# Layer 1's weighted sums in four column groups of TensorE, and the keys' loads on ScalarE's queue

## The chip, the cores and the metric

The kernel runs on one core of a Trainium2 chip. The metric is device time in microseconds (us), from one execution; the median of several is compared. Engines in the text: TensorE (PE in the profile; its weight loads are PEld), VectorE (DVE), ScalarE (ACT), GpSimd (POOL), SyncE (SP). A name with a q (SPq, ACTq) is that engine's sequencer, which issues DMAs.

## The reference

Two graph layers in fp32 over 16 graphs of 1024 nodes with 256 features. `adj` is an int32 matrix of 1024 x 1024 for each graph, zeros and ones here. Cut to what matters:

```python
h = relu(layernorm(x))
# layer 0: 8 heads of 32 features
Q, K, V = h @ Wq.T + bq, h @ Wk.T + bk, h @ Wv.T + bv       # split into heads
scores = where(adj == 0, -inf, Q @ K.T * 32 ** -0.5)          # per head, 1024 x 1024
x = x + concat(softmax(scores) @ V) @ Wo.T + bo
# layer 1: one head; adj chooses one of four edge vectors a_0 to a_3
h = relu(layernorm(x))
e_k = leaky_relu((h * a_k) @ h.T, 0.2)
scores = where(adj == 1, e_0, ..., where(adj == 4, e_3, -9e15))
x = x + softmax(scores) @ h
```

Layer 1's last line is what the change is about: for 128 queries at a time, probabilities (128 queries x 1024 nodes) times node features (1024 x 256), then a division by each query's sum and the residual.

## The kernel before

The work is cut into 128 blocks of 128 queries (16 graphs x 8 blocks). The main loop runs over steps `s`, one block each, and inside a step over the 8 heads `h`. A step carries several blocks at different stages at once, as a pipeline written out by hand (the order in the source is the order on every engine):

- `now` and `was` (class `Attend`): layer 0 of block `s`, and the end of block `s - 1`. For each head: scores on TensorE (L400, an fp32r matmul), the running maximum on VectorE (L412), the exponential on ScalarE (L420), then a turn of the probabilities so that nodes lie on partitions. Heads 1, 3, 5, 7 are turned by TensorE transposes (L512) and ScalarE copies (L513), heads 0, 2, 4, 6 by VectorE in 32 x 32 blocks (L345) and four DMAs that place the blocks (`placed`, L350). `combine` (L455) then sums the values, four heads at a time in four column groups of TensorE, each writing 32 partitions of `sums_place`; `combined` (L465) divides, `output` (L470) is the last matmul of layer 0, `residual` (L476) adds x and starts the norm, whose small steps run on GpSimd (L145 to L161); `normed` (L491) and `turn_normed` (L498, L502) make layer 1's features.
- `edge` and `edge_was` (class `Edges`): layer 1 of a block nine steps behind. `score` (L541), maximum and exponential, `turn_blocks` and `place_blocks` (VectorE and four DMAs into `pT1`, one buffer), then, one step later, `gather` (L581). Here the features are TensorE's weights and the turned probabilities stream, so the sums come out with features on partitions: `gathered` (L588) copies them to SBUF on ScalarE, `turn_back` (L593) turns them with two transposes into `brief`, and `store` (L597 to L600) divides, adds x and writes out, one step later still (`edge_last`).
- `piece`, `piece_was` (class `Piece`): keys, queries and values of a block nine steps ahead. `turn` (L224) transposes its features into `brief`, `turned` (L236, L237) copies them to SBUF twice on ScalarE, `project` (L254) makes keys and queries, `high` (L270, ScalarE) and `split` (L275, VectorE) cut them into two parts that go to DRAM (`write_keys` L299, `qd` L292).

Four places of 128 x 256 fp32 in PSUM are shared by hand. They are the halves of two banks: `sums_place` and `brief` in one, `early` and `late` in the other. Semaphores are put in by the framework, so that accesses to one bank by different engines follow the order of the source:

```python
banks = [ps_acc.tile([P, 2, D], F32, tag=f"acc{i}", ...) for i in range(2)]
sums_place, brief, early, late = (banks[i // 2][:, i % 2, :] for i in range(4))
```

The keys of a graph are 8 tiles of 128 x 1024 (one for each head), each in one buffer. `load_key` (L329) fetches them from DRAM: those of heads 0 to 5 of the next graph in the last step of a graph, two heads after their last use, those of heads 6 and 7 in the first step of the new graph. These DMAs, and nearly all others, are issued by SyncE; ScalarE issues the second copy of the keys' halves (`write_keys(1)`). After the loop a few small instructions test whether the graph has edges of kinds other than 1, for which a general path exists that these inputs do not take.

Of the kernel before, what the change touches and what calls it, by code (L numbers as in the profile page):

```python
# [42 lines left out]
def gnn_kernel(  # L43
# [42 lines left out]
    sums_place, brief, early, late = (banks[i // 2][:, i % 2, :] for i in range(4))  # L86
    sums_place = by_chunk(sums_place)

# [83 lines left out]
    class Piece:  # L172
# [42 lines left out]
        def turn(self):  # L215
            self.hT = self.buffer(2, [P, NC, self.n * P])
            self.hTm = self.buffer(4, [P, NC, self.n * P])
            for c in range(NC):
                if self.n > 1:
                    tr = ps_tr.tile([P, self.n, P], F32, tag="tr", name="trn0")  # L220
                elif c == 0:
                    tr = by_chunk(brief)
                for t in range(self.n):
                    nc.tensor.transpose(  # L224
                        tr[:, c if self.n == 1 else t, :], self.h[:, t, c * P : (c + 1) * P], ident
                    )
                if self.n > 1:
                    nc.scalar.copy(self.hT[:, c, :], tr.rearrange("p t n -> p (t n)"))
                    nc.vector.tensor_copy(
                        self.hTm[:, c, :].rearrange("p (t k b) -> p t k b", t=self.n, b=NB),  # L230
                        tr.rearrange("p t (b k) -> p t k b", b=NB),
                    )
            self.h_ps = tr
# [92 lines left out]
    def load_key(b, h):  # L326
        kt = keys.tile([P, N], F32R, tag=f"k{h}", name=f"k{h}_{b}")
        c, r = divmod(h, GROUP)
        nc.sync.dma_start(  # L329
            out=kt.bitcast(F32),  # L330
# [28 lines left out]
    class Attend:  # L359
# [87 lines left out]
        def turned_reciprocals(self):  # L447
            self.recT = work.tile([P, NC, P], F32, tag="cT", name="recT", bufs=1)
            nc.scalar.copy(self.recT, self.rec_ps)

        def combine(self, g):
            for j in range(NT):
                for r in range(GROUP):
                    h = g * GROUP + r
                    nc.tensor.matmul(  # L455
                        sums_place[r * HD : (r + 1) * HD, g, :],
                        lhsT=vs[self.b][:, j, place_of(h) : place_of(h) + HD],
# [5 lines left out]
        def combined(self):  # L463
            self.oT = work.tile([P, NC, P], F32, tag="oT")
            nc.vector.tensor_tensor(self.oT, sums_place, self.recT, ALU.mult)  # L465

# [49 lines left out]
    class Edges:  # L516
# [60 lines left out]

        def gather(self, c):

            for j in range(NT):  # L580
                nc.tensor.matmul(  # L581
                    sums_place[:, c, :], lhsT=h1s[self.b][:, j, c * P : (c + 1) * P], rhs=self.pT[:, j],
                    start=(j == 0), stop=(j == NT - 1),
                )

        def gathered(self):
            self.o1T = work.tile([P, NC, P], F32, tag="cT", name="o1T", bufs=1)
            nc.scalar.copy(self.o1T, sums_place)  # L588

        def turn_back(self):  # L590
            self.o = brief
            for c in range(NC):
                nc.tensor.transpose(self.o[:, c * P : (c + 1) * P], self.o1T[:, c, :], ident)  # L593

        def store(self):
            rec = small.tile([P, 1], F32, tag="rec1")
            nc.vector.reciprocal(rec, self.total)  # L597
            ot = work.tile([P, D], F32, tag="ot")
            nc.vector.scalar_tensor_tensor(ot, self.o, rec, self.x1, ALU.mult, ALU.add)  # L599
            nc.sync.dma_start(out=out[self.b, self.rows, :], in_=ot)  # L600
# [79 lines left out]
    with tc.manual_schedule():  # L680
# [21 lines left out]
        for piece in first:  # L702
            piece.values()
        piece, edge, edge_was, edge_last = piece_next, None, None, None
        now.load_queries()
# [10 lines left out]
        for s in range(B * NT + LAG + 1):  # L716
            b, t = divmod(s, NT)
            nxt, edge_nxt, piece_nxt = attend_of(s + 1), edges_of(s + 1), piece_of(s + 1)
            for h in range(HEADS):
# [4 lines left out]
                if now:  # L724
                    now.scores(h)
                    if h >= 2 and t == NT - 1 and b + 1 < B:
                        load_key(b + 1, h - 2)
                    if h < 2 and t == 0 and b > 0:
                        load_key(b, HEADS - 2 + h)
                if h == 0 and piece_was:  # L730
                    piece_was.split()
                if h == 1 and edge_last:
                    edge_last.store()
                if h == 1 and piece_was:
# [11 lines left out]
                if h == 6 and piece_was:  # L746
                    piece_was.split()
                    piece_was.split()
                if now:
                    now.softmax_max(h)  # L750


                if h == 7 and edge_was:
                    edge_was.gathered()
                if ending:
# [3 lines left out]
                if h == 7 and was:  # L759
                    was.normed()  # L760


                if h == 5 and piece:
                    piece.turn()
                if turning and th in BY_BLOCKS:
# [41 lines left out]
                if h == 4:  # L807
# [9 lines left out]
                    if edge_nxt:  # L817
                        edge_nxt.prepare()
                if h == 5:
                    if edge_was:  # L820
                        edge_was.gather(0)
# [15 lines left out]
                if h == 7:  # L837
                    if now:
                        now.combine(0)
                    if edge_nxt:  # L840
                        edge_nxt.mask()
                    if edge_was:
                        edge_was.turn_back()
                    if edge:
# [7 lines left out]
            gone, was, now = was, now, nxt  # L852
            edge_last, edge_was, edge = edge_was, edge, edge_nxt
            piece_was, piece = piece, piece_nxt

        edge_last.store()

# [51 lines left out]
```

## Time and profile before

| | us |
|---|---|
| median of 3 runs | 3425.91 (3419.38 to 3431.87) |
| profiled execution, its own time | 3418.87 |
| its span, first to last instruction | 3417.0 |
| busy: TensorE, VectorE, ScalarE, GpSimd | 3107.9, 2777.9, 2449.8, 2176.1 |
| DMA | 829.70 MB, mean 243 GB/s |
| mean granted TensorE clock | 0.979 |

A line of the page's groups reads: line, engine, operation, out<-in by the program's names, partitions x elements and type, how many; then after the bar the busy time of all in us and the mean of one in ns; after the next bar the idle time of the engine just before them, with what ended most of it. A row of the timeline is: start in us from the span's beginning, length in us, engine, line, operation, how many merged into the row, and in brackets the idle time ahead of it. fp32 matmuls appear as two records each, one for each pass over the data.

### The profile page before, as it was taken

To read this page: it belongs to the slowest core of one execution; us is meant where nothing else is said; L and a number is where in the kernel's file an instruction comes from. 1 tells how busy PE (TensorE), PEld (TensorE's weight loads), DVE (VectorE), ACT (ScalarE), POOL (GpSimd) and SP (SyncE) were. 2 spreads that over 40 slices of the span, in tenths; PEclk is the share of its full clock that TensorE was granted. 3 is DMA by queue.
4 is the path that set the end of the run, shared out by engine and by line. 5 is a ranking of instruction groups with operands and counts; after the bars stand their busy time and mean duration, and the time that the engine had idled before them with its cause. 6 is when DMAs were issued, how large, how long until landed. Compare 5 with 4: busy or idle time off the path is not lost. (4 is left out here: it accounts for less than half of the span.)

```text
span 3417.0 us, 92640 instructions
## 1 busy us (share of the span) xinstructions
PE 3107.9 (91%) x32178; PEld 2474.1 (72%) x32178; DVE 2777.9 (81%) x5111; ACT 2449.8 (72%) x4957; POOL 2176.1 (64%) x5274
## 2 busy tenths in 40 slices
PE   5778989899999999999899898999999999898987
PEld 3666777777777777777777777777777777776765
DVE  3778878788787888888888787888878788788873
ACT  3777777677676777767777676777767777777761
POOL 2456767667666766767667666766766666665553
PEclk8999999999999999999999999999999999999999
DMA  6778888888888888888888888888888888888764
GB/s 222 210 234 237 237 265 245 267 237 250 262 238 263 248 262 247 241 268 246 266 238 249 264 235 265 247 262 245 242 264 241 273 237 241 270 235 263 205 180 112
DMA packets 855754, 829.70 MB, mean 243 GB/s; under 512 B 73840, under 2 KB 804080, under 8 KB 855280
## 3 DMA queue, kind: packets, MB, share of 16 engines
q1 hardware_dynamic: 786800, 788.02, 77.1%
q10 hardware_dynamic: 68480, 35.67, 3.5%
q8 instruction: 260, 4.26, 0.5%
q14 instruction: 214, 1.75, 0.2%
HBM read 320.08 MB, written 167.77 MB: 143 GB/s over the span
## 5 line engine op out<-in xcount | busy, mean ns | idle before, releaser
L420 ACT ACTIVATE p<-p,nmx 128x1024 f32<-128x1024 f32 x1024 | 1181.2, 1154 | 361.1 <-DVE nmx L412 356.6
L412 DVE CUSTOM_DVE_ANT_0 p<-s,neg 128x1024 f32<-128x1024 f32 x1024 | 1242.7, 1214 | 193.6 <-PE s L400 172.3
L400 PE MATMUL s<-k,qt 128*128 128x512 f32 x2048 | 775.4, 460 | 24.9 <-DVE nmx L412 17.8
L455 PE MATMUL acc<-pT,v 128*32 128x128 f32 x16384 | 560.9, 281 | 91.7 <-DMA pT<-blocks 89.6
L345 DVE STREAM_TRANSPOSE blocks<-p 128x1024 f32<-128x1024 f32 x512 | 634.9, 1240 | 0.0
L382 POOL TENSOR_SCALAR neg<-adj 128x1024 bf16<-128x1024 int32 x128 | 467.9, 3655 | 213.9 <-DMA adj<-in_adj 210.9
L581 PE MATMUL acc<-pT,h 128*128 128x128 f32 x4096 | 512.1, 279 | 80.4 <-ACT hTm L237 68.4
L455 PEld LDWEIGHTS acc<-pT,v 128*32 128x32 f32 x16384 | 469.2, 113 | 155.7 <-issue 144.7
L581 PEld LDWEIGHTS acc<-pT,h 128*128 128x128 f32 x4096 | 480.0, 193 | 135.0 <-ACT hTm L237 115.9
L513 ACT COPY pT<-trp 128x512 f32<-128x512 f32 x1024 | 540.4, 578 | 33.4 <-DMA kd<-halves 18.2
L512 PE MATMUL trp<-ident,p 128*128 128x128 f32 x4096 | 537.7, 275 | 18.5 <-ACT p L420 17.7
L512 PEld LDWEIGHTS trp<-ident,p 128*128 128x128 f32 x4096 | 472.6, 141 | 90.8 <-ACT p L420 47.1
L535 POOL TENSOR_SCALAR neg<-adj 128x1024 bf16<-128x1024 int32 x128 | 469.2, 3666 | 39.9 <-DMA adj<-in_adj 30.4
L541 PE MATMUL s<-h1T,ha 128*128 128x512 f32 x1024 | 480.3, 592 | 0.5 <-ACT h1T L502 0.5
L400 PEld LDWEIGHTS s<-k,qt 128*128 128x128 f32 x2048 | 329.2, 192 | 141.1 <-DVE nmx L412 74.2
L439 POOL COPY wide<-rec 128x256 f32<-128x256 f32 x128 | 50.8, 397 | 520.5 <-DVE rec L437 487.6
L155 POOL TENSOR_TENSOR sq<-r 128x1 f32<-128x1 f32 (+1 forms) x750 | 247.5, 330 | 60.5
L541 PEld LDWEIGHTS s<-h1T,ha 128*128 128x128 f32 x1024 | 184.0, 190 | 136.9 <-issue 123.7
L554 DVE CUSTOM_DVE_ANT_0 sel<-s,neg 128x1024 f32<-128x1024 f32 x128 | 156.8, 1225 | 63.8 <-PE s L541 53.8
L420 ACT ACTIVATION_READ_ACCUMULATOR p<-p,nmx 128x1 f32 x1024 | 201.2, 197 | 0.0
L157 POOL TENSOR_SCALAR sq<-sq 128x1 f32<-128x1 f32 (+1 forms) x750 | 158.4, 211 | 65.7
L158 POOL TENSOR_TENSOR r<-r,sq 128x1 f32<-128x1 f32 (+1 forms) x750 | 151.0, 201 | 62.5
(104 smaller groups left out, 3952.6 us busy)
## 6 DMA issues: line engine op xcount, KB each, us to landing
pT<-blocks SPq DMA_DIRECT2D x2560, 128.0 KB, 3.2
adj<-in_adj SPq DMA_DIRECT2D x256, 512.0 KB, 5.2
qt<-qd SPq DMA_DIRECT2D x128, 512.0 KB, 6.3
k<-kd SPq DMA_DIRECT2D x128, 512.0 KB, 5.9
qd<-halves SPq DMA_DIRECT2D x240, 256.0 KB, 2.9
kd<-halves ACTq DMA_DIRECT2D x240, 128.0 KB, 3.0
kd<-halves SPq DMA_DIRECT2D x240, 128.0 KB, 2.6
xb<-in_x SPq DMA_DIRECT2D x128, 128.0 KB, 2.6
```

Of the source, the lines that this page charges most:

```text
L155: g.tensor_tensor(sq, r, r, ALU.mult)
L345: nc.vector.transpose(blocks.rearrange("p b j q -> p j b q"), p)
L382: nc.gpsimd.tensor_scalar(self.neg, self.adj, 0.0, MASKED, ALU.is_equal, ALU.mult)
L400: nc.tensor.matmul(self.ps[:, cols], lhsT=self.qt[:, h, :], rhs=keysets[self.b][h][:, cols], start=True, stop=True,)
L412: nc.vector.tensor_tensor_reduce(out=p, in0=sides[h in (3, 5, 7)], in1=self.neg, scale=-SCALE, scalar=FLOOR, op0=ALU.add, op1=ALU.min, acc ...
L420: nc.scalar.activation(p, p, AF.Exp, bias=nmx, scale=-1.0, accum_out=self.sums[:, h : h + 1])
L455: nc.tensor.matmul(sums_place[r * HD : (r + 1) * HD, g, :], lhsT=vs[self.b][:, j, place_of(h) : place_of(h) + HD], rhs=self.turned[h][:, j ...
L512: nc.tensor.transpose(tr[:, j, :], p[:, jj * P : (jj + 1) * P], ident)
L513: copy(pT[:, half * 4 : half * 4 + 4, :], tr)
L535: nc.gpsimd.tensor_scalar(self.neg, self.adj, 0.0, MASKED, ALU.is_equal, ALU.mult)
L541: nc.tensor.matmul(self.e[:, cols], lhsT=self.ha[:, c, :], rhs=h1Ts[self.b][:, c, cols], start=(c == 0), stop=(c == NC - 1),)
L581: nc.tensor.matmul(sums_place[:, c, :], lhsT=h1s[self.b][:, j, c * P : (c + 1) * P], rhs=self.pT[:, j], start=(j == 0), stop=(j == NT - 1),)
```

## The change

Layer 1's `gather` now takes the turned probabilities as weights, 32 queries for each of TensorE's four column groups, and streams the features, 256 columns at a time. The sums come out with queries on partitions, straight in `sums_place`. The two calls no longer take one half of the features each, but one half of the nodes each. `gathered` and `turn_back` go, and `store` reads `sums_place` in the same step (head 7, ahead of VectorE's maximum) where it read `brief` in the next one (head 1). `Piece.turn` for the pieces of the main loop writes to `late` where it wrote to `brief`, and comes behind the head's transposes at head 5 where it came ahead of them. `load_key` issues from ScalarE's queue, behind the head's exponential, and each key comes one head later: heads 0 to 4 in the last step of a graph, heads 5 to 7 in the first step of the next. The reciprocals' tile `recT` has a buffer of its own.

```diff
     sums_place, brief, early, late = (banks[i // 2][:, i % 2, :] for i in range(4))
-    sums_place = by_chunk(sums_place)
...
                 elif c == 0:
-                    tr = by_chunk(brief)
+                    tr = by_chunk(late)
                 for t in range(self.n):
...
         c, r = divmod(h, GROUP)
-        nc.sync.dma_start(
+        nc.scalar.dma_start(
             out=kt.bitcast(F32),
...
         def turned_reciprocals(self):
-            self.recT = work.tile([P, NC, P], F32, tag="cT", name="recT", bufs=1)
+            self.recT = work.tile([P, NC, P], F32, tag="recT", bufs=1)
             nc.scalar.copy(self.recT, self.rec_ps)
...
                     nc.tensor.matmul(
-                        sums_place[r * HD : (r + 1) * HD, g, :],
+                        sums_place[r * HD : (r + 1) * HD, g * P : (g + 1) * P],
                         lhsT=vs[self.b][:, j, place_of(h) : place_of(h) + HD],
...
             self.oT = work.tile([P, NC, P], F32, tag="oT")
-            nc.vector.tensor_tensor(self.oT, sums_place, self.recT, ALU.mult)
+            nc.vector.tensor_tensor(self.oT, by_chunk(sums_place), self.recT, ALU.mult)
...
-        def gather(self, c):
-
-            for j in range(NT):
-                nc.tensor.matmul(
-                    sums_place[:, c, :], lhsT=h1s[self.b][:, j, c * P : (c + 1) * P], rhs=self.pT[:, j],
-                    start=(j == 0), stop=(j == NT - 1),
-                )
-
-        def gathered(self):
-            self.o1T = work.tile([P, NC, P], F32, tag="cT", name="o1T", bufs=1)
-            nc.scalar.copy(self.o1T, sums_place)
-
-        def turn_back(self):
-            self.o = brief
-            for c in range(NC):
-                nc.tensor.transpose(self.o[:, c * P : (c + 1) * P], self.o1T[:, c, :], ident)
+        def gather(self, half):
+
+            for j in range(half * NT // 2, (half + 1) * NT // 2):
+                for a in range(NB):
+                    nc.tensor.matmul(
+                        sums_place[a * HD : (a + 1) * HD, :], lhsT=self.pT[:, j, a], rhs=h1s[self.b][:, j, :],
+                        start=(j == 0), stop=(j == NT - 1),
+                    )
...
             ot = work.tile([P, D], F32, tag="ot")
-            nc.vector.scalar_tensor_tensor(ot, self.o, rec, self.x1, ALU.mult, ALU.add)
+            nc.vector.scalar_tensor_tensor(ot, sums_place, rec, self.x1, ALU.mult, ALU.add)
             nc.sync.dma_start(out=out[self.b, self.rows, :], in_=ot)
...
             piece.values()
-        piece, edge, edge_was, edge_last = piece_next, None, None, None
+        piece, edge, edge_was = piece_next, None, None
         now.load_queries()
...
                     now.scores(h)
-                    if h >= 2 and t == NT - 1 and b + 1 < B:
-                        load_key(b + 1, h - 2)
-                    if h < 2 and t == 0 and b > 0:
-                        load_key(b, HEADS - 2 + h)
                 if h == 0 and piece_was:
                     piece_was.split()
-                if h == 1 and edge_last:
-                    edge_last.store()
                 if h == 1 and piece_was:
...
                     piece_was.split()
+                if h == 7 and edge_was:
+                    edge_was.store()
                 if now:
...
-                if h == 7 and edge_was:
-                    edge_was.gathered()
                 if ending:
...
-
-                if h == 5 and piece:
-                    piece.turn()
+                if now and h >= 3 and t == NT - 1 and b + 1 < B:
+                    load_key(b + 1, h - 3)
+                if now and h < 3 and t == 0 and b > 0:
+                    load_key(b, HEADS - 3 + h)
+
+
                 if turning and th in BY_BLOCKS:
...
                 if h == 5:
+                    if piece:
+                        piece.turn()
                     if edge_was:
...
                         edge_nxt.mask()
-                    if edge_was:
-                        edge_was.turn_back()
                     if edge:
...
             gone, was, now = was, now, nxt
-            edge_last, edge_was, edge = edge_was, edge, edge_nxt
+            edge_was, edge = edge, edge_nxt
             piece_was, piece = piece, piece_nxt
-
-        edge_last.store()
...
         seen = small.tile([P, B], F32, tag="seen", bufs=1)
```

## The prediction

> **What bounds the kernel now.** I read the page first, then the waits, then TensorE's timeline over two ordinary steps, then a step at which the graph changes. The page and the list of waits (who waited for whom: us in total, times, longest):
>
> ```profile
> PE 3107.9 (91%) x32178; PEld 2474.1 (72%) x32178; DVE 2777.9 (81%) x5111; ACT 2449.8 (72%) x4957; POOL 2176.1 (64%) x5274
> L455 PE MATMUL acc<-pT,v 128*32 128x128 f32 x16384 | 560.9, 281 | 91.7 <-DMA pT<-blocks 89.6
> L581 PE MATMUL acc<-pT,h 128*128 128x128 f32 x4096 | 512.1, 279 | 80.4 <-ACT hTm L237 68.4
> k<-kd SPq DMA_DIRECT2D x128, 512.0 KB, 5.9
> ACT o1T L588 <- PE acc L581: 148.8, 127, 11.4
> PE acc L581 <- ACT hTm L237: 68.4, 109, 0.7
> PE acc L455 <- DMA pT<-blocks: 89.6, 51, 5.2
> ```
>
> TensorE is nearly always busy. Matmuls are pipelined, so I price them from start to start in the timeline (start, us, then what runs, and in brackets the idle time before it):
>
> ```profile
> 1610.63 1.88 PE L541 MATMUL s<-h1T,ha 128*128 128x512 f32 x4
> ...
> 1619.37 1.13 PE L470 MATMUL acc<-woT,oT 128*128 128x256 f32 x4 [0.32 <-DVE oT L465]
> 1620.14 0.82 PE L400 MATMUL s<-k,qt 128*128 128x512 f32 x2
> 1620.86 0.44 PE L224 MATMUL acc<-ident,h 128*128 128x128 f32 x2
> 1621.14 1.04 PE L512 MATMUL trp<-ident,p 128*128 128x128 f32 x8
> 1622.01 1.95 PE L581 MATMUL acc<-pT,h 128*128 128x128 f32 x16
> 1623.72 0.71 PE L400 MATMUL s<-k,qt 128*128 128x512 f32 x2
> 1625.12 2.05 PE L581 MATMUL acc<-pT,h 128*128 128x128 f32 x16 [0.69 <-ACT hTm L237]
> 1627.02 1.06 PE L254 MATMUL acc<-hT,wkT 128*128 128x128 f32 x8
> ...
> 1629.34 1.96 PE L455 MATMUL acc<-pT,v 128*32 128x128 f32 x64
> 1631.22 0.44 PE L593 MATMUL acc<-ident,o1T 128*128 128x128 f32 x2
> 1631.41 0.71 PE L400 MATMUL s<-k,qt 128*128 128x512 f32 x2
> ...
> 1635.23 1.88 PE L541 MATMUL s<-h1T,ha 128*128 128x512 f32 x4
> ```
>
> A step is 24.60 us (1610.63 to 1635.23), and in it TensorE idles about 1.0: 0.32 for VectorE, 0.69 ahead of the second gather. The first step of a new graph is longer. The same row starts at 1477.09 and again, a step later, at 1508.48: 31.39 us. In between stands this:
>
> ```profile
> 1486.06 0.41 PE L455 MATMUL acc<-pT,v 128*32 128x128 f32 x4
> 1490.27 3.63 PE L455 MATMUL acc<-pT,v 128*32 128x128 f32 x60 [3.80 <-DMA pT<-blocks]
> ```
>
> Over the 15 such steps the starts of the first maximum (L412) give 98 us more than 15 times 24.6. VectorE had turned head 6 by 1479.79; SyncE issued its four placing DMAs only at 1485.39 to 1487.87, behind key loads and waits for landings. So two things bound the kernel: TensorE in ordinary steps, SyncE's queue and the DMAs at the change of graph.
>
> **What the Trainium skill says.** The Trainium skill, "PSUM — Partial Sum Buffer", section "PSUM bank collisions raise a hardware error": two engines must be kept apart by bank and quadrant, not by address. The trace agrees: `sums_place` and `brief` are halves of one bank, and the second gather waits 0.69 us for a ScalarE copy out of `brief` that it needs no data from. The Trainium skill, "TensorEngine Tiling (Array Packing)", Key Properties: changing the tiling mode drains the array. Around L455 the trace agrees: its quads of four column groups start 109 ns apart, but about 0.09 us is lost on the way in and 0.11 on the way out. The Trainium skill, "DMA: Bandwidth & Descriptors", Issuing engines are not separate DMA queues: another issuing engine saves its sequencer's time alone, since all use the same 16 DMA engines. The trace has no key on ScalarE's queue. The Trainium skill, "TensorE: Matmul & The Clock Gate", Part 1: after some 3.4 us of idleness the clock halves. It does here: 0.59 and 0.56 granted in the two stretches of 4 us from 1488, and the 60 matmuls above took 3.63 instead of about 1.9 us.
>
> **The change, part by part.** All in the ordinary step first.
>
> - The gather. Before, 16 matmul records of 128 columns took 1.71 us (1622.01 to 1623.72), 107 ns each. After, a half has 4 blocks by 4 groups by 2 passes, 32 records of 256 columns, in 8 quads. L455 shows that four groups of fp32 run together at the price of one (109 against 107), so a quad of 256 columns costs 2 x 107 + 2 = 216 ns, and a half 1.73, with 0.2 for entry and exit 1.93. That is +0.22 for each, against the undisturbed 1.71. Bounds: 1.71 if the switch hides, 2.15 if it costs twice as much or quads space out; never near four times, as L455 excludes serial groups.
> - `turn_back` (L593) goes: 1631.22 to 1631.41, -0.19. ScalarE's copy L588 goes (0.37) with its stall (148.8 / 127 = 1.17 each). ScalarE then waits there for GpSimd's `shift` (124.6 us in the list already), so I count nothing for it.
> - The false wait goes: the second gather shares no bank with `late`. Its -0.69 and the restart (1.90 instead of 1.71, -0.19) are gained. hT must now be ready for L254 only, and its copies end at 1625.07, before the new gather does.
> - `piece.turn` (L224) goes behind the transposes, into `late`, which VectorE's residual (L476, 1621.53 to 1621.92) must have read. TensorE gets there at 1621.73: a new wait of 0.2 to 0.3, with the gather and head 6's scores queued behind it. ScalarE's `high` comes at 1623.91, later than all this.
> - The store (0.12 + 0.48 us of VectorE) moves from head 1 to head 7. There VectorE idles 1.09 ahead of L412 for scores, so it is covered; it ends near 1628.0, before the next L455 needs its bank (1629.07). At head 1 it only lengthens VectorE's wait for L541 (0.31). Its DMA is the same one, earlier in SyncE's order.
>
> In order from 1610.63: L470 stays at +8.74 (VectorE sets it), L512 at +10.23, L224 at +11.4, gather +11.7 to +13.6, scores to +14.2, gather to +16.1, L254 +16.9, L400 +17.4, L512 +18.4, L455 +20.3, then 3.8 to the next L541: 24.1. Gain 0.5 per step, 0 to 0.8 with the bounds. GpSimd's own loop (VectorE's reciprocals, 16.7 us of GpSimd, 2 of ScalarE, VectorE's head 0 and 1) is some 24.1 us now and loses the store's 0.6: it doesn't become the bound. Over some 110 steps: **-55** (0 to -88).
>
> The keys. SyncE loses 8 issues of about 0.65 us at each change of graph, 5.2 in all, about what it was late. If head 6's DMAs go 3 to 4 us earlier, up to the 3.8 wait and the 1.7 of slow clock come back, 5.5. But both queues' DMAs carry eight semaphores in turn, and each waits for the landing of the DMA eight before it in program order. ScalarE's sequencer then holds all that is behind it:
>
> ```profile
> 1637.74 0.52 ACTq L299 DMA_DIRECT2D kd<-halves  x1
> 1638.46 1.07 ACT L513 COPY pT<-trp 128x512 f32<-128x512 f32 x2 [1.72 <-DMA pT<-blocks]
> ```
>
> Counting the new order, key 1 waits for `qt` (1.6 us of ScalarE, of which VectorE's idle 1.1 for `halves` hides most), and key 4 for key 3 itself: 5.9 to land, less 2.8 between two exponentials, 3.1, of which 1.5 is hidden by VectorE's idle time at head 0. Cost some 2.1, up to 5.7 if nothing hides. The issues themselves (0.5 each) lie beside a running exponential of 1.15. Net 5.5 - 2.1 = 3.4 at best; since the DMA engines are 0.97 busy there and the bytes stay, I take 2: 15 x 2 = **-30** (+60 to -75).
>
> The end loses L588, L593 and their hand-overs, -1.
>
> Sum: -55 - 30 - 1 = -86, against the profiled execution's 3418.87 us: 3333. That execution lies 7 us below the median of the runs shown (3425.91), so I say 3340.
>
> **Rivals.**
> - Only TensorE's part counts; the DMA engines set the change of graph as before. For it: 0.97 busy from 1458 to 1500. 3425.9 - 56 = 3370.
> - Only the keys count; TensorE's switches cost the full bound and a VectorE or GpSimd chain takes the rest. For it: VectorE has no idle time from 1612.66 to 1623.71. 3425.9 - 31 = 3395, and if the keys help little too, no change.
> - Slower: key loads hold ScalarE. Each change of graph pays 5.7 and SyncE's relief doesn't reach TensorE, since the blocks placed still wait for eight-deep landings. 15 x 5.7 = 86, less 35 of a smaller TensorE gain: +51, 3477. It decides from about 3.7 us per change of graph (55 / 15). For it: the 1.72 above, and 3.37 us of ScalarE idle at 1480.05 behind such an issue. Against it: GpSimd holds ScalarE at head 7 anyway.
>
> **How the numbers follow.** The forecast gets 0.42, the first rival 0.15, the second 0.15 (0.1 of it no change), the slower one 0.28. A measurement of this kernel can tell about 0.3%, 10 us, from no change. Faster 0.42 + 0.15 + 0.05 = 0.62, same 0.10, slower 0.28. The forecast's own range is 3290 to 3385; to leave out no more than 2 in 10 it must reach into the slower case: 3275 to 3445.
>
> **What would show it.** Right: the gather's row with 8192 records of 128*32 and 128x256, a half taking 1.85 to 2.0 us from start to start, no wait of it for L237; a step of about 24.1; the first step of a graph under 30; L455's waits for pT under 50 us in total. Wrong: halves above 2.15; a step still of 24.6; a new wait of ScalarE behind `k<-kd` issues above 60 us in total, with VectorE waiting for ScalarE's `halves` or exponentials in the last step of a graph.

## The result and the profile after: slower

The changed kernel takes 3547.57 us (median, 3546.29 to 3553.22), the kernel before, run beside it, 3427.92 (3419.38 to 3431.87): a ratio of 1.0356, with a 95% interval of 1.0332 to 1.0379. The forecast was 3340, and the result lies above its whole range. The span went from 3417.0 to 3546.5 us.

Lines of the changed kernel are mostly one lower than before (L412 is now L411, L513 is L512, L237 is L236). First the lines of its page that answer to those shown of before:

```profile
PE 3166.9 (89%) x36018; PEld 2259.1 (64%) x36018; DVE 2783.2 (78%) x5111; ACT 2418.5 (68%) x4829; POOL 2177.0 (61%) x5274
L454 PE MATMUL acc<-pT,v 128*32 128x128 f32 x16384 | 558.0, 284 | 18.6 <-DMA pT<-blocks 9.8
L581 PE MATMUL acc<-h,pT 128*32 128x256 f32 x8192 | 518.3, 388 | 11.1 <-DMA pT<-blocks 9.9
k<-kd ACTq DMA_DIRECT2D x128, 512.0 KB, 6.1
```

The edits did what they say. The gather has 8192 records of 128x256 in column groups and no wait for ScalarE's copy of hT; the keys go out on ScalarE's queue; and TensorE's waits of L455 for placed blocks fell from 89.6 to 9.8 us. Yet the run is longer. The list of waits of the changed kernel (who waited for whom: us in total, times, longest) shows what came in their place:

```profile
POOL neg L381 <- DMA adj<-in_adj: 274.8, 120, 14.7
ACT h L490 <- POOL shift L160: 185.0, 100, 13.0
PE trp L511 <- ACT p L419: 174.0, 107, 5.5
DVE halves L274 <- ACT hTm L236: 163.1, 119, 6.9
ACT pT L512 <- DMA pT<-blocks: 110.2, 40, 4.9
ACT pT L512 <- DMA kd<-halves: 81.1, 63, 2.8
```

(`hTm` is one of ScalarE's two copies of layer 0's turned features, `halves` are the parts of keys and queries, `kd<-halves` is a key write, `trp` and `pT` are turned probabilities before and after ScalarE's copy.) In the kernel before, these waits read:

```profile
POOL neg L382 <- DMA adj<-in_adj: 210.9, 93, 11.1
ACT h L491 <- POOL shift L161: 124.6, 120, 3.0
PE trp L512 <- ACT p L420: 17.7, 33, 1.4
ACT pT L513 <- DMA pT<-blocks: 6.8, 7, 1.7
ACT pT L513 <- DMA kd<-halves: 18.2, 38, 1.1
```

VectorE had no wait for hTm. TensorE's wait for it (68.4) is gone, and VectorE has one of 163.1, while its wait for ScalarE's `halves` fell from 149.7 to 61.2. TensorE's wait for exponentials is ten times what it was.

I measure a step from the start of one block's first maximum (L412, L411) to the next block's, and take apart three kinds (means, in us). The table adds up to the span's 129.5:

| | before | after | times | sum |
|---|---|---|---|---|
| ordinary step | 24.53 | 24.97 | 90 | +40 |
| last step of a graph | 25.71 | 28.44 | 14 | +38 |
| first step of a graph | 31.34 | 33.49 | 14 | +30 |
| the start: from the span's beginning to the first maximum | 70.6 | 79.8 | 1 | +9 |
| first nine steps together | 206.1 | 209.5 | 1 | +3 |
| the tail: from the last layer-0 step's start to the end | 133.8 | 142.6 | 1 | +9 |

The last and first steps of a graph are where the eight keys are loaded. ScalarE's timeline there (start, us, what runs, idle time before it in brackets):

```profile
1525.38 0.33 ACTq L328 DMA_DIRECT2D k<-kd  x1
1525.81 0.60 ACT L209 ACTIVATE h<-xin,shift,r 128x256 f32<-128x256 f32 x1 [4.63 <-DMA pT<-blocks]
...
1541.20 0.52 ACTq L298 DMA_DIRECT2D kd<-halves  x1
1541.88 0.51 ACTq L328 DMA_DIRECT2D k<-kd  x1
1542.42 0.37 ACT L501 COPY h1T<-acc 128x256 f32<-128x256 f32 x1 [4.67 <-PE s L540]
...
1548.21 0.52 ACTq L298 DMA_DIRECT2D kd<-halves  x1
1548.77 0.67 ACTq L328 DMA_DIRECT2D k<-kd  x1
1549.61 0.59 ACT L512 COPY pT<-trp 128x512 f32<-128x512 f32 x1 [4.54 <-DMA pT<-blocks]
```

Key 1 could be issued only at 1525.38, when `qt`, issued by SyncE at 1517.16 and eight DMAs ahead in program order, had landed (1525.36). ScalarE stood still for 4.63 us (the label names a placed block; what stands ahead of L209 in ScalarE's order is the key); over the 14 last steps it stands still there for 3.9 us on average. In the first step of the new graph it is mainly the second key write that holds ScalarE, twice. The one at 1541.20 waits for a block's DMA that lands at 1541.12, the one at 1548.21 for the write eight DMAs ahead, issued by SyncE at 1542.96, which lands only at 1548.13, among the keys. The key that is issued right behind each write adds 0.7 and 0.9 us. TensorE's timeline shows who paid:

```profile
1551.87 1.97 PE L511 MATMUL trp<-ident,p 128*128 128x128 f32 x8 [5.19 <-ACT p L419]
```

In such first steps TensorE waits 4.65 us on average for a ScalarE exponential; before, it waited 4.33 for placed blocks. So that wait is gone, one as long and of another cause stands in its place, and a wait in the last step came on top.

### The profile page after: what moved, and what is told of

Read it like the earlier page. It is cut to its first block, busy times and chain, and to the rows that moved or that the text cites. A ratio compares the mean times of both kernels' runs of the same rounds, so it can differ in the third digit from the quotient of the medians.

```text
span 3546.5 us, 100243 instructions
## 1 busy us (share of the span) xinstructions
PE 3166.9 (89%) x36018; PEld 2259.1 (64%) x36018; DVE 2783.2 (78%) x5111; ACT 2418.5 (68%) x4829; POOL 2177.0 (61%) x5274
## 5 line engine op out<-in xcount | busy, mean ns | idle before, releaser
L419 ACT ACTIVATE p<-p,nmx 128x1024 f32<-128x1024 f32 x1024 | 1183.1, 1155 | 309.1 <-DVE nmx L411 308.2
L411 DVE CUSTOM_DVE_ANT_0 p<-s,neg 128x1024 f32<-128x1024 f32 x1024 | 1242.1, 1213 | 88.5 <-PE s L399 73.9
L399 PE MATMUL s<-k,qt 128*128 128x512 f32 x2048 | 797.1, 471 | 57.1 <-DVE nmx L411 43.4
L511 PE MATMUL trp<-ident,p 128*128 128x128 f32 x4096 | 555.6, 280 | 174.1 <-ACT p L419 174.0
L512 ACT COPY pT<-trp 128x512 f32<-128x512 f32 x1024 | 546.3, 584 | 230.4 <-DMA pT<-blocks 110.2
L511 PEld LDWEIGHTS trp<-ident,p 128*128 128x128 f32 x4096 | 485.3, 144 | 278.7 <-ACT p L419 224.4
L454 PE MATMUL acc<-pT,v 128*32 128x128 f32 x16384 | 558.0, 284 | 18.6 <-DMA pT<-blocks 9.8
L581 PE MATMUL acc<-h,pT 128*32 128x256 f32 x8192 | 518.3, 388 | 11.1 <-DMA pT<-blocks 9.9
L454 PEld LDWEIGHTS acc<-pT,v 128*32 128x32 f32 x16384 | 470.8, 114 | 83.1 <-issue 57.0
L581 PEld LDWEIGHTS acc<-h,pT 128*32 128x32 f32 x8192 | 248.3, 111 | 232.3 <-issue 87.2
L156 POOL TENSOR_SCALAR sq<-sq 128x1 f32<-128x1 f32 (+1 forms) x750 | 246.1, 328 | 65.5
L274 DVE SCALAR_TENSOR_TENSOR halves<-acc,bq_t,halves 128x128 fp32r<-128x128 f32 x240 | 73.2, 346 | 167.0 <-ACT hTm L236 163.1
L490 ACT ACTIVATE h<-x,shift,r 128x256 f32<-128x256 f32 x128 | 76.6, 598 | 185.1 <-POOL shift L160 185.0
L419 ACT ACTIVATION_READ_ACCUMULATOR p<-p,nmx 128x1 f32 x1024 | 202.8, 198 | 0.0
## 6 DMA issues: line engine op xcount, KB each, us to landing
pT<-blocks SPq DMA_DIRECT2D x2560, 128.0 KB, 3.2
kd<-halves SPq DMA_DIRECT2D x240, 128.0 KB, 2.5
kd<-halves ACTq DMA_DIRECT2D x240, 128.0 KB, 2.9
xb<-in_x SPq DMA_DIRECT2D x128, 128.0 KB, 2.7
```

Source lines behind the costliest of these rows:

```text
L156: g.tensor_scalar(sq, sq, 1.5, None, ALU.add)
L399: nc.tensor.matmul(self.ps[:, cols], lhsT=self.qt[:, h, :], rhs=keysets[self.b][h][:, cols], start=True, stop=True,)
L411: nc.vector.tensor_tensor_reduce(out=p, in0=sides[h in (3, 5, 7)], in1=self.neg, scale=-SCALE, scalar=FLOOR, op0=ALU.add, op1=ALU.min, acc ...
L419: nc.scalar.activation(p, p, AF.Exp, bias=nmx, scale=-1.0, accum_out=self.sums[:, h : h + 1])
L454: nc.tensor.matmul(sums_place[r * HD : (r + 1) * HD, g * P : (g + 1) * P], lhsT=vs[self.b][:, j, place_of(h) : place_of(h) + HD], rhs=self ...
L511: nc.tensor.transpose(tr[:, j, :], p[:, jj * P : (jj + 1) * P], ident)
```

## The experiments

The prediction had a sum of parts, so I took the parts off one by one. "Step" below is the ordinary step. Each run has its own runs of the kernel before on the same chip; the ratios are against those.

**e1_keys_syncE**: the changed kernel, keys back on SyncE and at their old heads.

```diff
-        nc.scalar.dma_start(
+        nc.sync.dma_start(
             out=kt.bitcast(F32),
```

> The changed kernel with the keys' loads back on SyncE's queue and in their old places (right behind the scores, one head earlier); the gather in column groups stays. Theory (the keys on ScalarE cost at the change of graph and at the start, nothing in between): the last and first step of a graph lose about 2 us each, the first scores come 9 us earlier, ordinary steps stay at 25.0 us; some 60 us below the changed kernel, 3480 to 3500. Rival (the change of graph is long because of the gather's order, whoever issues the keys): 3530 to 3550, and the last and first steps stay at 28.4 and 33.5.

3482.74 us, ratio 1.0166 (1.0143 to 1.0190). The last step of a graph falls to 26.34, the first to 31.73, the start to 70.9; the ordinary step stays at 24.96, the tail at 143.4. So the keys account for 65 us of the loss, as expected.

**e2_keys_only**: the reverse, the kernel before with its keys on ScalarE's queue, one head later.

> The kernel before with only the keys' loads moved to ScalarE's queue and one head later. Theory: slower than before by 50 to 80 us, all of it in the start (+9), the last step of a graph (+2 to 3 each) and the first (+2 each); ScalarE shows waits for qt, x and pT landings behind k<-kd issues; ordinary steps stay at 24.5. Rival (the keys are harmless alone and hurt only together with the new order of the gather): within 15 us of before.

3477.22 us, ratio 1.0150 (1.0126 to 1.0173), so +54 by the keys alone. The last step of a graph grows to 29.23, the start to 78.8; the first step of a graph, which I expected to grow by 2, stays (31.39). Its list of waits has TensorE behind ScalarE here too:

```profile
PE trp L512 <- ACT p L420: 78.8, 40, 5.6
```

against 17.7 before: the new wait, without any column group.

**e3_out_late** and **e4_keys_and_out**: the store's result goes out in head 1 of the next step, as before the change, while VectorE's store itself stays at head 7. e3 has this alone, e4 also has the keys of e1.

```diff
             nc.vector.scalar_tensor_tensor(ot, sums_place, rec, self.x1, ALU.mult, ALU.add)
-            nc.sync.dma_start(out=out[self.b, self.rows, :], in_=ot)
+            self.ot = ot              # edge_last.send() issues it at h == 1
```

> The changed kernel with the DMA that writes the output issued where it was before (head 1 of the next step); the store's two VectorE instructions stay at head 7. Theory (the write-out ahead of the placing of layer 1's blocks makes SyncE late, so that ScalarE's write of the keys' halves at head 1 waits for the landing of a placing DMA eight issues before it, and holds the exponential that TensorE's transposes at head 3 need): the wait of the transposes for ScalarE falls from 1.0 us per ordinary step to 0.2, the step from 25.0 to about 24.2, the tail loses about 9 us; 3440 to 3470. Rival (the step is set by the column groups or by VectorE's wait for the copies of hT in the same bank): steps stay at 24.8 to 25.0, 3530 to 3550.

> Both at once: keys on SyncE in their old places, and the output's DMA at head 1 of the next step. What is left of the change is the gather in column groups, the store's place on VectorE and the turn into the other bank. Theory: ordinary steps about 24.1 to 24.2 against 24.5 before, the change of graph and the start as before: 3370 to 3400, faster than before. Rival (column groups or the bank order cost the step): 3430 to 3460, slower than before.

e3: 3502.03 us, 1.0222 (1.0188 to 1.0257); step 24.68. e4: 3451.42, 1.0086 (1.0063 to 1.0108); step 24.64. One DMA, the same one, was worth 45 us beside the keys' new place (3547.6 to 3502.0) and 31 beside the old (3482.7 to 3451.4). At head 7 it stands in SyncE's order ahead of layer 1's placing DMAs and must wait for the gather and the store. ScalarE's second key write at head 1 waits for the landing of the DMA eight before it, which is one of those placing DMAs, and holds ScalarE's copies; TensorE's L511 waits for p fall from 174.0 in the changed kernel to these, first in e3, then in e4:

```profile
PE trp L511 <- ACT p L419: 106.9, 79, 4.6
PE trp L511 <- ACT p L419: 54.2, 73, 2.0
```

Both runs stay well above what I expected: the step fell by 0.3, not by 0.8. The keys took 65 us, this DMA 31, and what is left to explain is e4's 28 us.

**f1_key_write_behind**, **f2_turn_ahead_of_store**, **f4_both_orders**: two orders in e4. f1 puts ScalarE's second key write behind its copies, f2 VectorE's turn of layer 1's blocks ahead of the store at head 7.

```diff
-                if h < 2 and piece_was:          # f1: now below the turns
-                    piece_was.write_keys(1)
+                if h == 7 and edge:              # f2
+                    edge.turn_blocks()
                 if h == 7 and edge_was:
                     edge_was.store()
```

> The changed kernel with the keys back on SyncE and the out DMA at head 1 (e4_keys_and_out, 3451 us), and in it ScalarE's key write of heads 0 and 1 put behind the two copies of transposed probabilities. Theory: this write waits for a landing and holds ScalarE's copies, so TensorE's transposes at head 3 wait 0.46 us per step for an exponential. Then that wait falls under 0.15, the ordinary step goes from 24.64 to 24.2 and the run to 3405 to 3420. Rival: another loop (VectorE with its two splits, or GpSimd with the shift of the norm and the mask) sets 24.6 anyway: the wait turns up elsewhere, and the run stays within 8 us of 3451.

> e4_keys_and_out (3451 us) with VectorE's turn of layer 1's blocks at head 7 put ahead of the store instead of behind it. Theory: in the last eight steps, where layer 1 is alone, the store waits for the gather's end and holds the turn of the next blocks, some 1.2 us a step; with the turn first the tail falls from 143 to about 134 us and the run to 3440 to 3445. In ordinary steps little changes (the store ends 1.2 us later, and the next sums need its bank: up to 0.2 us a step, 20 us, against it). Rival: the tail is long since the gather in column groups now needs each placing DMA one by one: tail still 142 to 144.

> Both edits of f1_key_write_behind and f2_turn_ahead_of_store together in e4_keys_and_out. If both theories hold: step 24.2, tail 134, run 3395 to 3412, under the kernel before (3424). If the loop of the other engines sets the step: 3440 to 3445, slower than before.

f1: 3454.71 us, 1.0088 (1.0071 to 1.0105), no gain: the wait for the landing now stands ahead of the exponential (40.3 us of L419 behind `kd<-halves`), and TensorE waits for p no less than in e4 (72.6). f2: 3474.24, 1.0142 (1.0125 to 1.0158). The tail fell by more than the theory has it, from 143.2 to 128.2. But the ordinary step went to 25.05, and the run is some 20 us longer than e4's, not 6 to 11 shorter, since the late store holds the bank of the next sums:

```profile
PE acc L454 <- DVE ot L590: 65.6, 117, 1.0
```

That is 0.56 us each time, in nearly every step, where I had priced at most 0.2. f4: 3485.98, 1.0163 (1.0140 to 1.0185), step 25.11: f2's price and nothing from f1.

**f3_piece_turn_alone**: the kernel before with the one edit that removes TensorE's false wait.

```diff
-                    tr = by_chunk(brief)
+                    tr = by_chunk(late)
@@ piece.turn() moves behind the transposes of p, ahead of the first gather half
```

> The kernel before with one part of the change alone: layer 0's two transposes of h go into late, behind the transposes of the probabilities, so that the second gather no longer shares a bank with what ScalarE copies out. No column groups, no change of the store or the keys. Theory: this removed wait is what the change really has to give: 0.69 of waiting and 0.19 of restart, less a new wait of 0.2 to 0.3 for VectorE's residual; step 24.53 to about 24.0, run 3360 to 3385. Rival: a loop of VectorE, ScalarE and GpSimd already stands close behind TensorE at 24.4 to 24.5: the freed time comes back as waits of TensorE for p and for oT, and the run is 3410 to 3430.

3441.33 us, 1.0048 (1.0031 to 1.0065): slower, by 16. This was the turning point, since the edit carries no column group, no key and no store. Its list of waits:

```profile
POOL neg L382 <- DMA adj<-in_adj: 258.6, 108, 9.0
ACT h L491 <- POOL shift L161: 215.3, 125, 3.2
DVE halves L275 <- ACT hTm L237: 132.7, 119, 1.4
```

TensorE's 68.4 us for hTm are gone, and VectorE, which had none, has 132.7 for the same copy. `late` shares its bank with `early`, which VectorE's splits of the queries read while ScalarE copies h out of `late`. The Trainium skill, "PSUM — Partial Sum Buffer", section "PSUM bank collisions raise a hardware error", says that engines are kept apart by bank and quadrant; this trace agrees, since the framework's semaphore orders two readers of different data. The false wait was moved, not removed. And GpSimd is behind. I read the chain of waits so: its mask waits for adj, its shift is late, ScalarE's L491 waits for the shift, and what follows on ScalarE makes VectorE and then GpSimd's next round late, a closed round of about 24.5 us. The next runs try this.

**g1_adj_earlier, g2_before_mask_later, g3_piece_turn_mask_later, g4_all_mask_later_tail**: they open this round. g1 is e4 with adj loaded at the end of head 0. The others move GpSimd's mask (3.66 us) behind the norm: g2 in the kernel before, g3 in f3, g4 in e4, with f2's order in the tail alone.

```diff
-                    if nxt:                      # head 3
-                        nxt.mask()
@@ end of head 5, behind was.residual() and piece.turned()
+                    if nxt:
+                        nxt.mask()
```

```diff
@@ g1: end of head 0 instead of head 1
+                    if nxt:
+                        nxt.load()
@@ g4 has also, at head 7
+                if h == 7 and edge and not now:
+                    edge.turn_blocks()
                 if h == 7 and edge_was:
                     edge_was.store()
```

> e4_keys_and_out (3451 us, ordinary step 24.64) with the load of the next adj issued at the end of head 0 instead of in head 1, so ahead of the out DMA and the second key write on SyncE. Theory: GpSimd's mask waits 1.80 us a step for adj, and a late mask makes the norm's shift late, which holds ScalarE at head 7, then VectorE's splits and maxima, and so the reciprocals with which GpSimd's next round begins. GpSimd's rounds of e4 without a wait for adj take 24.07 us, with over 1.5 us of it 25.07. With adj some 1.3 us earlier the wait falls under 1 us, the step to 24.3 and the run to 3410 to 3430. Rival: adj lands as late as before, since it waits for the landing eight DMAs before it or shares the engines with the placing DMAs: wait 1.5 to 2 us, run within 8 us of 3451.

> The kernel before with one GpSimd instruction moved: the mask of the next step's layer 0 (3.66 us, waits for adj) goes behind the norm of x1, from head 3 to the end of head 5. Then the shift doesn't wait for adj any more, and comes some 1 us earlier. Theory: in the kernel before TensorE with its wait for hTm (0.59 and the restart) and GpSimd's round both take 24.5; freeing GpSimd alone leaves TensorE's: 3405 to 3430, step 24.4 to 24.6. Rival: GpSimd's round was the only bound before, and TensorE's wait for hTm is a part of it: step under 24.2, run under 3390.

> f3_piece_turn_alone (3441 us, step 24.70) with GpSimd's mask behind the norm as in g2_before_mask_later. Theory: with both bounds removed, the false wait of TensorE and GpSimd's round, the step falls to 23.9 to 24.1 and the run to 3350 to 3375, the gain that the change's own edit at TensorE had to give. Rival: VectorE's splits, which now wait for ScalarE's copy out of the same bank (1.08 us a step), are a third bound: step 24.4 to 24.6, run 3405 to 3430.

> e4_keys_and_out with GpSimd's mask behind the norm, and with VectorE's turn of layer 1's blocks ahead of the store in the steps without layer 0 alone (where f2_turn_ahead_of_store took 15 us off the tail; in ordinary steps it cost 0.55 a step). The column groups stay. Theory: step 24.0 to 24.2, since TensorE's own work was as forecast, tail 128 to 130, run 3375 to 3395, faster than before; some 10 to 20 us behind g3_piece_turn_mask_later, since the column groups cost TensorE 0.15 a half and save turn_back's 0.19. Rival: VectorE's splits or the longer halves set the step at 24.5: run 3425 to 3435.

g1: 3438.11 us, 1.0046 (1.0029 to 1.0062); the wait for adj fell from 1.80 to 0.81 us a step and the step to 24.46, the run 8 us above what I expected. g2: 3424.87, 1.0003 (0.9993 to 1.0013). ScalarE's waits for the shift fell from 124.6 to 10.9, and nothing was gained; TensorE still waits for hTm:

```profile
ACT h L491 <- POOL shift L161: 10.9, 18, 2.3
PE acc L581 <- ACT hTm L237: 65.6, 109, 0.7
```

g3: 3418.81, 0.9988 (0.9974 to 1.0001): both opened, and still no gain clear of the noise, as its rival has it. g4: 3437.49, 1.0044 (1.0027 to 1.0062), step 24.53 and tail 128.0, a little beyond its rival's range.

**h1_groups_alone, h2_hT_copies_later, h4_key_writes_sync**: three edits of g3, each alone.

```diff
@@ h1: gather in column groups; ScalarE copies the sums as they lie, VectorE stores at head 1
-            nc.scalar.copy(self.o1T, sums_place)
+            nc.scalar.copy(self.o, banks[0][:, 0, :])
@@ h2: head 5 to head 6, behind that head's exponential
-                    if piece:
-                        piece.turned()
@@ h4: second key write
-            (nc.sync, nc.scalar)[twice].dma_start(
+            (nc.sync, nc.scalar if self.n > 1 else nc.sync)[twice].dma_start(
```

> g3_piece_turn_mask_later (3419 us, ordinary step 24.40, tail 135.8) with the gather in column groups as its one further edit: ScalarE copies the sums as they lie at head 7, VectorE stores at head 1 as in the kernel before, and turn_back goes. So the groups are priced without the store's move. Theory: TensorE loses 0.15 in each half and gains turn_back's 0.19, +0.1 a step; the rest of the step is ScalarE's and VectorE's; step 24.4 to 24.5, tail 132 to 136, run 3415 to 3432. Rival: the switches of the mode cost more than the halves show, also ahead of the scores behind each half: step 24.7 to 24.8, run 3450 to 3465.

> g3_piece_turn_mask_later with ScalarE's two copies of layer 0's transposed h behind the exponential of head 6 instead of ahead of it, so that VectorE's two splits, which read the other half of the same bank, don't wait for them (0.95 us a step). Theory: VectorE is the loop that sets the step together with ScalarE: step 24.1 to 24.2, run 3390 to 3402. Rival: that wait has slack behind it (VectorE waits 0.89 a step for scores anyway), and the hT copies come too late for the projection L254: step 24.4 to 24.6, run 3415 to 3440.

> g3_piece_turn_mask_later with the second key write of heads 0 and 1 issued by SyncE right behind the first, not by ScalarE; the number and order of bytes stay. ScalarE then never waits for a landing in an ordinary step. Theory: that wait (0.74 + 0.17 us a step ahead of ScalarE's copies) is what now makes TensorE wait 0.76 for p at head 3; the wait of TensorE falls under 0.2, step 23.8 to 24.0, run 3350 to 3375. Rival: SyncE, which issues in 0.79 of its time, takes 1.2 us more a step and puts the placing DMAs and adj later: TensorE waits for pT instead, step 24.4 to 24.8, run 3420 to 3460.

h1: 3441.92 us, 1.0050 (1.0033 to 1.0066), between its theory and its rival and 23 above g3, though the tail gave back 5: step 24.66 against 24.40. The idle time of TensorE in the step is less (0.95 against 1.09), so its own work grew by 0.40. One sees where by laying TensorE's timeline of the changed kernel beside g3's. The changed kernel:

```profile
1612.03 0.38 PE L223 MATMUL acc<-ident,h 128*128 128x128 f32 x2
1612.34 1.93 PE L581 MATMUL acc<-h,pT 128*32 128x256 f32 x32
1614.20 0.73 PE L399 MATMUL s<-k,qt 128*128 128x512 f32 x2
1614.87 1.93 PE L581 MATMUL acc<-h,pT 128*32 128x256 f32 x32
1616.73 1.16 PE L253 MATMUL acc<-hT,wkT 128*128 128x128 f32 x8
1617.64 0.71 PE L399 MATMUL s<-k,qt 128*128 128x512 f32 x2
```

and g3, with the gather of before and no wait in it:

```profile
1802.48 0.38 PE L224 MATMUL acc<-ident,h 128*128 128x128 f32 x2
1802.70 1.95 PE L581 MATMUL acc<-pT,h 128*128 128x128 f32 x16
1804.40 0.71 PE L400 MATMUL s<-k,qt 128*128 128x512 f32 x2
1804.95 1.95 PE L581 MATMUL acc<-pT,h 128*128 128x128 f32 x16
1806.73 1.06 PE L254 MATMUL acc<-hT,wkT 128*128 128x128 f32 x8
1807.55 0.71 PE L400 MATMUL s<-k,qt 128*128 128x512 f32 x2
```

From start to start the five rows take 0.31, 1.86, 0.67, 1.86 and 0.91 against 0.22, 1.70, 0.55, 1.78 and 0.82; the medians over all ordinary steps of h1 and g3 are within 0.01 of these. The halves themselves cost +0.16 and +0.08, and the rows before and behind them +0.30 together. The sum is +0.54, less `turn_back`'s 0.19. It is not the quads: inside a half of the changed kernel they start 216 ns apart, so that eight of them are 1.73. What is added is the way in and out.

h2: 3406.24 us, 0.9943 (0.9926 to 0.9961), step 24.17: faster than both kernels, though a little above what I expected. VectorE's splits don't wait for hTm any more, and in ordinary steps ScalarE's copies are early enough for the projection. In the first steps, where layer 1 doesn't run yet, they are not: TensorE waits 28.4 us for them in all, and the first nine steps take 217.0 against g3's 210.6. h4: 3457.74, 1.0088 (1.0062 to 1.0114). TensorE's wait for p is gone from the list, as the theory has it, but SyncE's two further issues a step make the placing DMAs late, as the rival has it:

```profile
PE acc L455 <- DMA pT<-blocks: 234.2, 132, 5.2
```

against 89.6 before. The last step of a graph, with SyncE's eight keys, is the worst: 29.36.

**i1_copies_later_mask_as_before, i2_changed_kernel_mended**: i1 is h2 with GpSimd's mask back at head 3; i2 is g4 with h2's edit, so the changed kernel with its column groups and store kept and everything around them mended. Both have

```diff
@@ head 5 to head 6
-                    if piece:
-                        piece.turned()
```

> h2_hT_copies_later (3406 us, step 24.17) with GpSimd's mask back at head 3. Tells whether both loops had to be opened. Theory: GpSimd's round with its wait for adj is again a bound: step 24.4 to 24.6, run 3420 to 3440. Rival: the false wait of the splits was the only thing that held the freed TensorE: step 24.1 to 24.2, run 3400 to 3412.

> g4_all_mask_later_tail (3437 us, step 24.53), so the changed kernel with the keys on SyncE, the out DMA at head 1, GpSimd's mask behind the norm and the turn ahead of the store in the tail, and now also ScalarE's copies of hT behind the exponential of head 6. Column groups stay. Theory: the last bound by another engine falls as in h2_hT_copies_later, and what stays is TensorE's own 0.4 us a step of the column groups: step 24.4 to 24.5, run 3425 to 3437, level with the kernel before or behind it. Rival: the groups' cost was hidden by VectorE's wait: step 24.2, run 3400 to 3412.

i1: 3423.32 us, 0.9996 (0.9982 to 1.0010), step 24.54: with the mask back, all of h2's gain is gone. The step is the upper end here, since the profiled execution (3434.13 us) was the slowest of twelve. i2: 3422.45, 0.9992 (0.9982 to 1.0003), step 24.45, tail 129.8: level with the kernel before, 16 behind h2. Its ordinary step is 0.28 longer than h2's, and TensorE's own work in it 0.40 longer (23.70 against 23.30), as between h1 and g3.

## Why the prediction was wrong

The forecast was -86 us, and the change was +120. Three terms of the sum failed. The gain of 0.5 a step, from the false wait, did not come, since the wait went to VectorE and GpSimd's round stood close behind. The keys, put at -30, cost 54 to 65. The store's DMA, put at nothing, cost 31 to 45.

- **The gather's price: the mechanism was right, the way in and out was mis-sized.** The quads start 216 ns apart, as forecast. For entry and exit I took 0.2 a half; with what the neighbouring rows pay it is 0.28. With `turn_back` gone, as predicted, I forecast +0.25 net a step; h1 against g3 shows 0.40. In the changed kernel TensorE's own work, the step less its idle time, went from 23.54 to 23.75 only, since the end of the false wait gave some back (23.31 in g3). That is 19 us over 90 ordinary steps, about half of their 40; the other half is waiting.
- **The false wait: the step that failed first.** I checked what TensorE would wait for in `late` (the residual: forecast 0.2 to 0.3 a step, measured 0.5 us in the whole run) and not who else uses the bank. VectorE's splits do. f3 shows the move for +16 us, h2 against g3 that this wait held 0.23 of the step.
- **"GpSimd's own loop … is some 24.1 us now … it doesn't become the bound": wrong.** The sum left out the mask's wait for adj, which was in the list with 210.9 us and which I passed over as an engine that isn't busy. i1 against h2 prices the mask's place at 17 us by the medians, and at 0.37 a step at most. The list of waits alone could have told: ScalarE's 124.6 us for the shift, which I took as a reason to count nothing for the copy L588, was the end of that loop, as I read it now.
- **The store: "Its DMA is the same one, earlier in SyncE's order", costed at nothing.** e3 measured 45 us, e1 against e4 31. I said what covers VectorE's part, not what waits behind the DMA on SyncE, nor what ScalarE waits for eight DMAs later.
- **The keys: rival three's mechanism, at its place.** I forecast -30 with SyncE's relief of 5.5 per graph against a hold of 2.1. The relief came (L454's waits for pT, 9.8), and the sign that I named for it, under 50, was met; but TensorE waits the same time for ScalarE instead. The hold was mis-sized: I reckoned `qt` with 1.6 us for key 1; it took 8.2 to land (1517.16 to 1525.36; the median of the 14 last steps is 8.2 too, against 6.35 before), a hold of 4.63. And I counted holds at keys only: with keys in flight the landings that the ordinary key writes wait for take 5 us too, and those writes, with the key behind each, hold ScalarE for 4.67 and 4.54 us in the first step. e1 and e2 put the keys at 54 to 65 us, of which the start is 8 to 9, below the 86 of the rival. (The 5.7 behind that 86 doesn't follow from its terms: 1.6 and 3.1 are 4.7, which gives 70.) The rival's other condition, "less 35 of a smaller TensorE gain", failed; so even the slower rival's 3477 was too low, by 70.
- **The start and the end.** The start I did not cost: +9, all of it the keys (e1 has 70.9). The end I put at -1: it was +9, since the store waits for the gather's end and VectorE's next turn stands behind it (f2 takes 15 off).

What stays open: e2 moves the keys' queue and their place by one head together, and the two were not told apart. ScalarE's wait for a landing ahead of its second key write (54.6 us still in h2) was moved in f1 and h4 but not removed without another cost. h2's last steps of a graph are 1.5 us longer than the kernel before's (27.24 against 25.71); TensorE waits 2.27 us there for placed blocks, against 1.20, and why these come later is not explained. GpSimd's closed round is read from the chain of waits; the runs show that the mask's place counts, not each link of the chain.

## What to carry to other kernels

When a false wait is removed by using another buffer, list every engine that touches the new buffer's bank, and close every engine's loop over a step with its waits for DMAs in it, not only its busy time: f3 and g2 freed one engine each, g3 and i1 two, and they lost or gained nothing clear of the noise, while h2 freed three and gained 19 us. With eight semaphores in turn, as here, an instruction that issues a DMA is a wait for an older landing placed on that engine; moving it earlier, or to a compute engine, puts that wait ahead of all that is queued there. A wait that vanishes from TensorE's list has to be looked for under another name before it is booked as gain.

## What the runs showed of the hardware that I had not expected

- Loads on a second queue made a transfer of the first one slower. At the start `qt` landed 7.25 us after its issue when the eight keys followed it on SyncE's queue, and 17.18 us after it with the keys on ScalarE's, though issued at the same time (60.75 and 60.71); two keys had been issued ahead of it, and seven of the eight landed ahead of it. The Trainium skill, "DMA: Bandwidth & Descriptors", Queues, rings and completion order, says that a DMA engine goes round the queues that have work for it and takes a whole packet from each. The trace agrees. `qt` moves in packets of 512 bytes and the keys in packets of 4096, and from 68 to 76 us of the changed kernel ScalarE's queue (q10) and SyncE's (q1) moved (packets, MB, share of the 16 engines' time):

```profile
q10 hardware_dynamic: 789, 2.88, 88.0%
q1 hardware_dynamic: 788, 0.40, 16.5%
```

One packet went for one packet, so the queue with the small packets got a seventh of the other's bytes. No run here changed the sizes.

- Four column groups of fp32 with 256 columns: a quad starts 216 ns after the one before it, where twice the 107 ns of one matmul of 128 columns is 214. The way into the groups and out of them costs about 0.28 us for a half of 32 matmuls, of which about half (0.15) shows in the rows of the neighbours.
- SyncE, which computes nothing, can be what TensorE waits for: its issues fill 0.79 of the main loop of the kernel before, and two issues more in each step (h4) cost 34 to 39 us against g3, with TensorE's wait for placed blocks at 234.2 us in all.
